# Two joins of a four-layer network in one kernel: 64-channel weights loaded early, evictions shared, transposes earlier, weight steps regrouped and wide idle products added

## The chip, the cores and the metric

The kernel runs on one core of a Trainium2 chip. The metric is the device time of one execution in microseconds (us). The core's engines are TensorE (PE in the profile; its weight loads are PEld), VectorE (DVE), ScalarE (ACT), GpSimd (POOL) and SyncE (SP); each works through its own list of instructions in order, and they wait for one another by semaphores. SP, ACT and POOL also issue DMA transfers (SPq, ACTq, POOLq).

## The reference

Everything is float32. The input x is 4 images of 256 channels, 56 x 56 pixels. Four residual layers follow one another; each normalises its input by groups (32 groups of 8 channels, per image) and adds its result to its input:

```python
x = x + involution0(groupnorm(x))   # h = reduce(x) 256 -> 64 channels; kernels = span(h), 16 groups of 7x7;
                                    # every pixel's 7x7 neighbourhood is weighted by its own kernels
x = x + conv(groupnorm(x))          # relu(n + bn2(conv3x3(relu(bn1(conv3x3(n))))))  with n = groupnorm(x)
x = x + involution2(groupnorm(x))   # as layer 0, with relu(bn(.)) on the 64 channels, relu(bn(.)) on the result
x = x + fourier_gates(groupnorm(x)) # n times a channel gate plus n times an image gate
```

## The kernel before

The program is one launch. `involution_layer(0)`, `conv_layer` and `involution_layer(2)` (which also does layer 3 image by image) are written one behind the other, each overlapping its end with the beginning of the next. Within a stage a function `in_order` fixes the order of instructions on each engine to that in which the Python code emits them, so an instruction waits behind everything emitted ahead of it on its engine. Small generators are stepped by hooks: `place(after, g, (1, 3, 5))` puts one step of `g` behind positions 1, 3 and 5 of a loop.

**An involution layer.** A 64-channel bottleneck comes first. `bottleneck(b)` (line 421) multiplies the 64-channel weights `red_sb` by the normalisation's scale (`redn`, line 430), finds a bias from them by a product with the shift (line 437) and an addition (`hb`, line 448), and then, for 7 pieces of 9 rows, makes products of 504 columns into one PSUM bank per pair of pieces (line 459): one piece of a pair lies in partitions 0 to 63, the other in 64 to 127. The evictions (line 478 in layer 2) are three ACT activations a piece, with relu, into `hp`; and as the taps need each piece in both halves of the partitions, a copy of 64 x 504 is made on DVE (line 467).

The tap stage (`tap_matrices`, line 569) makes the 7 x 7 weights: groups of 12 records (products of 133 columns, line 580) into two banks, evicted in turn by ACT (line 591, one group in three) and DVE (line 598, two in three) with a bias into `kt`. `z_sb` and `zb_sb` are tables for these products, read back from memory at the beginning of layer 2 (lines 952, 953). The windows `xw` of the image are made beside them: `next_strip` (line 362) writes a normalised strip (line 379 by ACT in layer 2, line 381 by POOL in layer 0), `begin_windows` (line 390) transposes it by 7 products with a unit matrix (line 396), and `next_windows` copies it out by ACT (line 408) and issues four DMAs by SP. Three windows are made ahead (`NXW = 3`), by hooks at groups 2, 7 and 12 of the first tap stage. `apply` (line 622) then multiplies taps and windows, and lines 635 to 647 evict that and add the residual.

**The convolution.** Both 3 x 3 convolutions are done in positions: along x a transform of the input turns 4 columns of output into 6 positions, taken in the order 1, 2, 3, 4, 0, 5. `phases` (line 1274) writes the input's normalised phases `ph` by ACT (line 1290, 8 of them), `input1` (and `input2` for the second convolution) with the transform (lines 1293 to 1320) compute `v`, one tile a position, on DVE: lines 1298 to 1302 end the first position, lines 1304 to 1320 the others; line 1318 ends the one that `conv2`'s first products wait for. `row_weights` (line 1201) makes the weights' positions on DVE, per half `ci` of the input channels: two additions (1218, 1219) and a subtraction (1220) for the first positions, three more operations (1223 to 1225) for the later ones; `u_sb` holds them. It runs as `weights1` for the first convolution (products in line 1411) and as `weights2` for the second (line 1493), the latter stepped at positions 3, 5, 7, 9 and 11 of the first chunk of `conv1`. DVE also evicts the products: lines 1432 to 1440 in `conv1`, 1503 to 1530 in `conv2`, the last piece of the convolution in lines 1524 to 1529.

**The first join.** At the end of layer 0, `begin_conv` (line 1145) issues the first rows of the convolution (`load_rows(0)`) and raw weights by SP. At the start of `conv_layer` (lines 1561 to 1580) TensorE makes 24 narrow products of 16 columns (`window_biases`, line 255), which are the biases of layer 2's taps; ACT copies them out and SP stores them (line 1570), then `load_rows(1)` issues four loads by SP (line 1137); DVE does the first `weights1` steps and the first `v`.

**The second join.** `begin_last` loads the first image of layer 2 into its blocks during the last steps of the convolution. `involution_layer(2)` issues the loads of `red_sb` by ACT (line 317) where the layer's tiles are made, `z_sb` and `zb_sb` by SP, then runs `bottleneck(0)` in one go, then the first strip and the taps.

Of the kernel before, what the change touches and what calls it, by code (L numbers as in the profile page):

```python
# [71 lines left out]
def net_kernel(  # L72
# [59 lines left out]
    for i in range(2):  # L132
        nc.scalar.dma_start(rp[i * R : (i + 1) * R, :], rpar)
    mhalf = const.tile([P, NB], F32, name="mhalf")
    nc.gpsimd.memset(mhalf, -0.5)
# [64 lines left out]
    def norm_steps(st, one_bank, layer, b, cb):  # L200
# [22 lines left out]
        yield  # L223

    def mark():
        return len(nc.cur_bb.bb.instructions)
# [22 lines left out]

    def window_biases(zb_sb, bias, ps):  # L250

        bias_f = bias[:G, KK * KK : KK * KK + ZN]
        for p in range(TP):
            z0 = ZF - p // TX * QX - p % TX
            nc.tensor.matmul(  # L255
                ps[:Q, p * G : (p + 1) * G],
                bias_f[:, z0 : z0 + Q],
                ident_sb[:G, :G],
                start=True,
                stop=True,  # L260
            )
        nc.scalar.copy(
            zb_sb.rearrange("q g p -> q p g"), ps[:Q, : TP * G].rearrange("q (p g) -> q p g", g=G)
        )
# [15 lines left out]
    def involution_layer(layer, xin, xout, red, span, sb, xs_of, ahead=None, pending=None):  # L280

        with ExitStack() as es:
# [23 lines left out]
            if layer == 0:  # L306
# [3 lines left out]
                nc.scalar.copy(norm_sb[:, 3, B - 1, 1, :], mhalf)  # L310

            red_sb = wpool.tile([P, NB, 2, R], F32, name="red_sb")

            def load_red():
                for i in range(2):
                    eng = nc.gpsimd if layer == 0 else nc.scalar
                    eng.dma_start(red_sb[:, :, i], red.rearrange("(cb p) r -> p cb r", p=P))

            if layer == 2:
                load_red()  # L320
            z_sb = wpool.tile([P, G // 2, ZN], F32, name="z_sb")
# [40 lines left out]
            def next_strip():  # L362
# [14 lines left out]
                img = xs_of[b, cb].rearrange("p (h w) -> p h w", w=W)[:, :, lo:hi]  # L377
                if layer == 2:
                    nc.scalar.activation(dst, img, AF.Identity, bias=shift, scale=rstd)
                else:  # L380
                    nc.gpsimd.tensor_scalar(dst, img, rstd, shift, ALU.mult, ALU.add)  # L381
# [39 lines left out]
            def bottleneck(b):  # L421
# [3 lines left out]

                rstd, shift = norms[layer][b]

                redn = work.tile([P, NB, 2, R], F32, name="redn", bufs=1)
                for ci in range(NB):
                    nc.vector.tensor_scalar_mul(redn[:, ci], red_sb[:, ci], rstd[:, ci : ci + 1])  # L430
                hp = new_h().rearrange("p (y x a t) -> p y x a t", y=TY, x=TX, t=NTX)
# [20 lines left out]
                for j in range(0, NH, 2):  # L452
                    halves = [slice(0, R), slice(R, P)] if j + 1 < NH else [slice(0, P)]
                    ps = one_bank()
                    for ci in range(NB):
                        for i, m in enumerate(halves):
# [8 lines left out]
                            )  # L465
                    for dst, part in copies:
                        nc.vector.tensor_copy(dst, part)
                    copies = []
                    s = ps[:, : ROWS_H * W].rearrange("p (a y t x) -> p y x a t", y=TY, t=NTX, x=TX)
                    for i, m in enumerate(halves):  # L470
                        rows = min(ROWS_H, H - (j + i) * ROWS_H)
                        a0, n = (j + i) * ROWS_H // TY, -(-rows // TY)
                        for py in range(min(rows, TY)):
                            dst = hp[m, py, :, a0 : a0 + n, :]
                            if layer == 0:
                                nc.scalar.activation(dst, s[m, py, :, :n, :], AF.Identity, bias=hb[m])
# [4 lines left out]
                        if len(halves) > 1:  # L481
                            part = hp[:, :, :, a0 : a0 + n, :].rearrange("p y x a t -> p (y x) (a t)")
                            copies.append((part[halves[1 - i]], part[m]))
                    yield

            def begin():
# [7 lines left out]
                next(tables)  # L494
                load_red()
                hp = new_h().rearrange("p (y x a t) -> p y x a t", y=TY, x=TX, t=NTX)
# [7 lines left out]
                sums0, sums1 = sums(0, 0), sums(0, 1)  # L504
                redn = work.tile([P, NB, 2, R], F32, name="redn", bufs=1)
                rstd, shift = norms[0][0]
# [443 lines left out]
            else:  # L950
                since = mark()
                nc.sync.dma_start(z_sb, z2_dram)
                nc.sync.dma_start(zb_sb, zb2_dram)
                run(bottleneck(0))
                hooks0[3] = list(pending[0])
            next_strip()
            for i in range(NXW):
                hooks0.setdefault(2 + 5 * i, []).extend((next_windows, next_strip))

# [185 lines left out]
    def begin_conv():  # L1145
        room["v2"] = new_block()
        load_rows(0, src[1])
        raw_weights(1, 0, 1, nc.sync)

    def begin_weights(part):  # L1150
# [4 lines left out]
    def conv_layer(xin, xout, st, ahead):  # L1155
        with ExitStack() as es:
# [44 lines left out]
            def row_weights(u, wc, raw=None):  # L1201
# [15 lines left out]
                for w0, w1, w2, u1, u2, u3, u4 in ws:  # L1217
                    tt(u2, w0, w2, ALU.add)
                    tt(u1, u2, w1, ALU.add)
                    tt(u2, u2, w1, ALU.subtract)  # L1220
                    yield
                for w0, w1, w2, u1, u2, u3, u4 in ws:
# [345 lines left out]
            zb2 = room["bias"][:Q, KK * KK + ZN : KK * KK + ZN + G * TP].rearrange("p (g t) -> p g t", g=G)  # L1568
            window_biases(zb2, room["bias"], one_bank())
            nc.sync.dma_start(zb2_dram, zb2)  # L1570
            load_rows(1, xin)
            g = input1(0)
            for _ in range(4):
                next(g)
            run(weights1)
            run(g)
# [73 lines left out]
    def begin_last():  # L1650
        for cb in range(NB):
            blocks[0, cb] = new_block()
            load_block(blocks[0, cb], src[2][0][cb])

    pending = conv_layer(src[1], src[2], st, begin_last)
# [66 lines left out]
```

## Time and profile before

| quantity | value |
|---|---|
| runs of the kernel before (us) | 1819.07, 1824.24, 1819.11, 1819.72; median 1819.42 |
| the profiled execution | 1819.07 us, of which 1817.3 from its first to its last instruction |
| busy share: PE, DVE, ACT, POOL | 95%, 76%, 46%, 24% |
| granted TensorE clock, mean | 0.98 of full speed |
| the first join | about 505 to 592 us |
| the second join | about 1239 to 1292 us |

The profile's times are us from the span's first instruction. Its views: the chain that ended last gives, in order of time, the start of a piece, its length and what it was (engine, tile, line, number of instructions); the timeline gives groups of instructions, with the idle time of the engine ahead of them and what ended it in square brackets; the windows give for a stretch each engine's busy time and the TensorE clock that was granted, as a share of full speed. A float32 product shows as several matmul records. Line numbers are those of the kernel before.

### The profile page before, as it was taken

What the parts mean: (1) busy time and instruction counts of PE and PEld (TensorE: products, weight loads), DVE (VectorE), ACT (ScalarE), POOL (GpSimd) and SP (SyncE); (2) the same over time, 40 slices, a digit from 0 to 9 for tenths busy, and PEclk for the clock granted to TensorE, in tenths of its full rate; (3) what the DMA queues carried; (4) which work ended last, traced back from release to release, by engine and by line L of the source; (5) the groups of instructions that cost most, each with busy time, mean ns of one, the idle gap of its engine ahead of it and who ended that gap; (6) DMA issues with size and microseconds to landing.
All of it is one profiled execution on the core that took longest, in us unless ns stands there. A gap on an engine that the chain in (4) does not pass through costs nothing.

```text
span 1817.3 us, 55835 instructions
## 1 busy us (share of the span) xinstructions
PE 1719.0 (95%) x24034; PEld 1512.1 (83%) x24034; DVE 1375.1 (76%) x2729; ACT 843.5 (46%) x1981; POOL 431.4 (24%) x626
## 2 busy tenths in 40 slices
PE   7999999999989999999999999996999899899897
PEld 6998889889878988998899889984987787787785
DVE  3787777776689988898888988874777577677675
ACT  3566556555533222322222212103767567577564
POOL 2333432245200000000000000000000465474582
PEclk9999999999989999999999999998999999999996
DMA  2545534454651101111111111131434566665653
GB/s 85 160 154 161 169 115 149 149 158 134 197 176 45 63 26 63 67 64 40 62 60 59 60 41 34 37 131 57 158 130 144 171 200 201 185 222 172 178 157 114
DMA packets 66004, 215.77 MB, mean 119 GB/s; under 512 B 13237, under 2 KB 20926, under 8 KB 62046
## 3 DMA queue, kind: packets, MB, share of 16 engines
q1 hardware_dynamic: 48718, 145.24, 25.3%
q0 software_dynamic: 14688, 64.78, 11.2%
q8 instruction: 190, 3.11, 0.7%
q10 hardware_dynamic: 2352, 2.18, 0.4%
q14 instruction: 56, 0.46, 0.1%
HBM read 76.30 MB, written 49.15 MB: 69 GB/s over the span
## 4 chain that ended last, share of the span: by engine, by line
PE 78%; DVE 8%; ACT 5%; DMA 4%; issue 2%; POOL 2%; SPq 1%; POOLq 0%; ACTq 0%; DVEq 0%
PE mm L1493 20%; PE ps L580 17%; PE ps L622 14%; PE mm L1411 10%; PE mm L1382 5%; PE ps L396 5%; DMA xw<-xw 3%; ACT kt L591 2%; PE ps L459 2%; DVE un L642 1%; DVE kt L598 1%; ACT xw L408 1%; PE ps L705 1%; PE ps L928 1%; PE ps L255 1%
## 5 line engine op out<-in xcount | busy, mean ns | idle before, releaser
L622 PE MATMUL ps<-kt,xw 126*32 126x48 f32 (+1 forms) x12544 | 378.2, 234 | 30.0 <-issue 20.7
L580 PE MATMUL ps<-hp,z_sb 64*126 64x133 f32 x6144 | 390.3, 281 | 16.1 <-ACT kt L591 8.2
L622 PEld LDWEIGHTS ps<-kt,xw 126*32 126x32 f32 (+1 forms) x12544 | 340.2, 121 | 74.8 <-issue 53.7
L580 PEld LDWEIGHTS ps<-hp,z_sb 64*126 64x126 f32 x6144 | 368.0, 187 | 33.8 <-ACT kt L591 14.4
L1493 PE MATMUL mm<-v,u_sb 128*128 128x280 f32 (+1 forms) x1728 | 385.0, 384 | 3.4 <-DVE v L1318 3.4
L598 DVE TENSOR_TENSOR kt<-ps,zb_sb 126x798 f32<-126x798 f32 x336 | 319.9, 982 | 89.9 <-PE ps L580 89.3
L1493 PEld LDWEIGHTS mm<-v,u_sb 128*128 128x128 f32 x1728 | 327.5, 190 | 57.9 <-DVE v L1318 3.8
L591 ACT ACTIVATE kt<-ps,zb_sb 126x133 f32<-126x133 f32 x1056 | 307.4, 444 | 93.7 <-PE ps L580 93.1
L1411 PE MATMUL mm<-v,u_sb 128*128 128x252 f32 (+1 forms) x936 | 212.0, 387 | 2.6 <-DVE v L1302 2.6
L1411 PEld LDWEIGHTS mm<-v,u_sb 128*128 128x128 f32 x936 | 177.8, 191 | 33.2 <-issue 2.6
L1530 POOL DMA_DIRECT2D x<-xs x24 | 13.1, 547 | 682.8 <-DVE xs L1529 427.3
L642 DVE SCALAR_TENSOR_TENSOR un<-ps,s,un 128x240 f32<-128x240 f32 x224 | 102.5, 457 | 88.2 <-ACT un L637 84.1
L642 DVE SCALAR_TENSOR_TENSOR un<-ps,par_sb,un 128x240 f32<-128x240 f32 x224 | 98.1, 457 | 87.2 <-ACT un L635 82.7
L1478 ACT ACTIVATE res<-xs,shift,norm_sb 128x1120 f32<-128x1120 f32 (+1 forms) x24 | 30.2, 1258 | 234.9 <-DVE xs L1529 107.2
L408 ACT COPY xw<-ps 126x896 f32<-126x896 f32 x112 | 101.5, 906 | 46.8 <-PE ps L396 37.5
L647 POOL TENSOR_TENSOR xs<-un,xs 128x240 f32<-128x240 f32 x112 | 72.3, 665 | 193.4 <-DVE un L642 193.4
L396 PE MATMUL ps<-ident_sb,strip_sb 128*126 128x128 f32 x784 | 110.6, 281 | 6.6 <-POOL strip_sb L381 6.1
L635 ACT ACTIVATE un<-ps,par_sb 128x240 f32<-128x240 f32 x112 | 50.2, 449 | 115.8 <-PE ps L622 113.8
L637 ACT ACTIVATE un<-ps,bn_t,s 128x240 f32<-128x240 f32 x112 | 60.2, 538 | 88.5 <-PE ps L622 79.6
L1382 PE MATMUL mm<-xs,u_sb 128*128 128x126 f32 (+1 forms) x792 | 98.5, 277 | 1.2 <-DVE xs L1345 0.9
L396 PEld LDWEIGHTS ps<-ident_sb,strip_sb 128*126 128x126 f32 x784 | 84.1, 141 | 17.5 <-POOL strip_sb L381 7.3
L139 POOL TENSOR_TENSOR norm_sb<-norm_sb,mhalf 128x1 f32<-128x1 f32 x32 | 19.8, 620 | 329.5 <-DVE norm_sb L138 329.5
(254 smaller groups left out, 2005.6 us busy)
## 6 DMA issues: line engine op xcount, KB each, us to landing
xw<-xw SPq DMA_DIRECT2D x168, 252.0 KB
xw<-xw SPq DMA_DIRECT2D x224, 126.0 KB
xw<-xw POOLq DMA_DIRECT2D x56, 252.0 KB, 4.7
xs<-x SPq DMA_DIRECT2D x24, 560.0 KB
x<-xs POOLq DMA_DIRECT2D x8, 1568.0 KB, 8.3
xs<-x SPq DMA_DIRECT2D x8, 1568.0 KB
xs<-in_x_dram SPq DMA_DIRECT2D x6, 1568.0 KB
x<-xs SPq DMA_DIRECT2D x6, 1568.0 KB
```

The costliest lines, as they stand in the source:

```text
L396: nc.tensor.transpose(ps[:Q, k * P : (k + 1) * P], flat[:, k * Q : (k + 1) * Q], ident_sb)
L408: nc.scalar.copy(xw[:, :NSB, :], ps[:Q, : NSB * P].rearrange("q (n c) -> q n c", n=NSB))
L580: nc.tensor.matmul(ps[:Q, i, k * NT : (k + 1) * NT], z_sb[i * R : (i + 1) * R, cb * GB // 2 + gp, z0 : z0 + Q], hp[i * R : (i + 1) * R, py ...
L591: nc.scalar.activation(kt[:, g0 + i, pb, :, k], ps[:Q, i, k * NT : (k + 1) * NT], AF.Identity, bias=zb_sb[:, cb * GB + g0 + i, p0 + k : p0 ...
L598: nc.vector.tensor_tensor(kt[:, g0 : g0 + 2, pb], ps[:Q, :, : PB * NT].rearrange("q i (k t) -> q i t k", k=PB), zb_sb[:, cb * GB + g0 : cb ...
L622: nc.tensor.matmul(v[m * j : m * j + m, i, :, k * TP : (k + 1) * TP], xw[:, window(ty), m * j : m * j + m], kt[:, ng * j : ng * j + ng, :, ...
L637: nc.scalar.activation(part, o[0], AF.Identity, bias=bn["t4"][:, cb : cb + 1], scale=bn["s4"][ng][:, 0, cb : cb + 1])
L642: nc.vector.scalar_tensor_tensor(part, o[e], s, part, ALU.mult, ALU.add)
L647: nc.gpsimd.tensor_tensor(dst, u, dst, ALU.add)
L1382: nc.tensor.matmul(ps[:, co * m : (co + 1) * m], u[ci][:, co * P : (co + 1) * P], v2[:, e, : n // 2, ci * WT : (ci + 1) * WT], start=(ci = ...
L1411: nc.tensor.matmul(ps, u1_sb[:, ci, dy, k, co * P : (co + 1) * P], v[:, k, dy * NB + ci : (dy + n - 1) * NB + ci + 1 : NB, :], start=(j == 0),
L1493: nc.tensor.matmul(ps, u2_sb[:, ci, dy, k, co * P : (co + 1) * P], v[:, k, dy * NB + ci : (dy + n - 1) * NB + ci + 1 : NB, :], start=(j == 0),
```

## The change

*Ahead of layer 2.* `red_sb` becomes a tile that lives for the whole program, filled for layer 2 by SP at the end of layer 0. Its scaling (`redn`) is done in `begin_last` during the convolution's last steps.

*Bottleneck of the first image of layer 2.* Of a pair of pieces, ACT evicts the first (three activations), DVE the second by three multiply-and-add operations and a maximum with zero. ACT makes one of the two copies, DVE the other.

*First windows of layer 2.* The first strip is written ahead of the bottleneck, and two of the three windows are transposed and copied between the bottleneck and the taps; the third stays at hook 7. The first two strips are made by POOL.

*Start of the convolution.* In `row_weights` both halves' first weights (additions) come first and both subtractions in a step of their own, behind the third step of the first `v`. Between the narrow bias products 12 wide ones of 448 columns are put, a unit matrix times rows of the input, into a bank that nobody reads. For `weights2` the step more means that its later operations move behind the `v` of the same position.

```diff
@@ -131,6 +131,16 @@
     rp = const.tile([P, 5], F32, name="rp")
     for i in range(2):
         nc.scalar.dma_start(rp[i * R : (i + 1) * R, :], rpar)
+
+    red_sb = const.tile([P, NB, 2, R], F32, name="red_sb")
+
+    def load_red(red, eng):
+        for i in range(2):
+            eng.dma_start(red_sb[:, :, i], red.rearrange("(cb p) r -> p cb r", p=P))
+
+    def new_redn():
+        return const.tile([P, NB, 2, R], F32, name="redn")
+
     mhalf = const.tile([P, NB], F32, name="mhalf")
     nc.gpsimd.memset(mhalf, -0.5)
 
@@ -222,6 +232,14 @@
         nc.vector.scalar_tensor_tensor(shift, gm, -1.0, rstd, ALU.mult, ALU.mult)
         yield
 
+    redn_of = {}
+
+    def norm_weights(layer, b):
+
+        redn = redn_of[layer, b] = new_redn()
+        for ci in range(NB):
+            nc.vector.tensor_scalar_mul(redn[:, ci], red_sb[:, ci], norms[layer][b][0][:, ci : ci + 1])
+
     def mark():
         return len(nc.cur_bb.bb.instructions)
 
@@ -247,7 +265,7 @@
         copy(field(bias_f), bias_g.rearrange("p (y x) -> p y x", y=KK))
         yield
 
-    def window_biases(zb_sb, bias, ps):
+    def window_biases(zb_sb, bias, ps, between=None):
 
         bias_f = bias[:G, KK * KK : KK * KK + ZN]
         for p in range(TP):
@@ -259,6 +277,8 @@
                 start=True,
                 stop=True,
             )
+            if between is not None and p % 2:
+                between()
         nc.scalar.copy(
             zb_sb.rearrange("q g p -> q p g"), ps[:Q, : TP * G].rearrange("q (p g) -> q p g", g=G)
         )
@@ -308,16 +328,6 @@
                 load(0, 1, (2, 2, 2, 1))
 
                 nc.scalar.copy(norm_sb[:, 3, B - 1, 1, :], mhalf)
-
-            red_sb = wpool.tile([P, NB, 2, R], F32, name="red_sb")
-
-            def load_red():
-                for i in range(2):
-                    eng = nc.gpsimd if layer == 0 else nc.scalar
-                    eng.dma_start(red_sb[:, :, i], red.rearrange("(cb p) r -> p cb r", p=P))
-
-            if layer == 2:
-                load_red()
@@ -375,7 +385,7 @@
                     nc.vector.memset(st[:, PAD : PAD + H, at + hi - lo : QX], 0.0)
                 dst = st[:, PAD : PAD + H, at : at + hi - lo]
                 img = xs_of[b, cb].rearrange("p (h w) -> p h w", w=W)[:, :, lo:hi]
-                if layer == 2:
+                if layer == 2 and len(strips) > 2:
                     nc.scalar.activation(dst, img, AF.Identity, bias=shift, scale=rstd)
                 else:
                     nc.gpsimd.tensor_scalar(dst, img, rstd, shift, ALU.mult, ALU.add)
@@ -423,11 +433,13 @@
 
 
 
-                rstd, shift = norms[layer][b]
-
-                redn = work.tile([P, NB, 2, R], F32, name="redn", bufs=1)
-                for ci in range(NB):
-                    nc.vector.tensor_scalar_mul(redn[:, ci], red_sb[:, ci], rstd[:, ci : ci + 1])
+                _, shift = norms[layer][b]
+
+                both = (layer, b) == (2, 0)
+
+                if (layer, b) not in redn_of:
+                    norm_weights(layer, b)
+                redn = redn_of[layer, b]
                 hp = new_h().rearrange("p (y x a t) -> p y x a t", y=TY, x=TX, t=NTX)
                 nc.gpsimd.memset(hp[:, TY - 1, :, NTY - 1, :], 0.0)
                 h_of[b] = hp
@@ -463,8 +475,11 @@
                                 start=(ci == 0),
                                 stop=(ci == NB - 1),
                             )
-                    for dst, part in copies:
-                        nc.vector.tensor_copy(dst, part)
+                    for i, (dst, part) in enumerate(copies):
+                        if both and i == 1:
+                            nc.scalar.copy(dst, part)
+                        else:
+                            nc.vector.tensor_copy(dst, part)
                     copies = []
                     s = ps[:, : ROWS_H * W].rearrange("p (a y t x) -> p y x a t", y=TY, t=NTX, x=TX)
                     for i, m in enumerate(halves):
@@ -472,7 +487,11 @@
                         a0, n = (j + i) * ROWS_H // TY, -(-rows // TY)
                         for py in range(min(rows, TY)):
                             dst = hp[m, py, :, a0 : a0 + n, :]
-                            if layer == 0:
+                            if both and i == 1:
+                                nc.vector.tensor_scalar(
+                                    dst, s[m, py, :, :n, :], bn["s3"][m], hb[m], ALU.mult, ALU.add
+                                )
+                            elif layer == 0:
                                 nc.scalar.activation(dst, s[m, py, :, :n, :], AF.Identity, bias=hb[m])
                             else:
                                 nc.scalar.activation(
@@ -481,6 +500,8 @@
                         if len(halves) > 1:
                             part = hp[:, :, :, a0 : a0 + n, :].rearrange("p y x a t -> p (y x) (a t)")
                             copies.append((part[halves[1 - i]], part[m]))
+                            if both and i == 1:
+                                nc.vector.tensor_scalar_max(part[m], part[m], 0.0)
                     yield
 
             def begin():
@@ -492,7 +513,7 @@
                 tables = span_table(z_sb, span, scratch, nc.gpsimd.dma_start, nc.scalar.copy)
                 next(biases)
                 next(tables)
-                load_red()
+                load_red(red, nc.gpsimd)
                 hp = new_h().rearrange("p (y x a t) -> p y x a t", y=TY, x=TX, t=NTX)
                 nc.gpsimd.memset(strip_sb, 0.0)
                 nc.gpsimd.memset(hp[:, TY - 1, :, NTY - 1, :], 0.0)
@@ -502,7 +523,7 @@
                 window_biases(zb_sb, scratch[:, n:], one_bank())
                 folds = batch_norms()
                 sums0, sums1 = sums(0, 0), sums(0, 1)
-                redn = work.tile([P, NB, 2, R], F32, name="redn", bufs=1)
+                redn = new_redn()
                 rstd, shift = norms[0][0]
                 steps(sums0, NCHUNK)
                 norm = norm_of(0, 0, 0, sums_of[0, 0])
@@ -951,11 +972,17 @@
                 since = mark()
                 nc.sync.dma_start(z_sb, z2_dram)
                 nc.sync.dma_start(zb_sb, zb2_dram)
+                next_strip()
                 run(bottleneck(0))
                 hooks0[3] = list(pending[0])
-            next_strip()
-            for i in range(NXW):
-                hooks0.setdefault(2 + 5 * i, []).extend((next_windows, next_strip))
+                for _ in range(NXW - 1):
+                    next_windows()
+                    next_strip()
+                hooks0[7] = [next_windows, next_strip]
+            if layer == 0:
+                next_strip()
+                for i in range(NXW):
+                    hooks0.setdefault(2 + 5 * i, []).extend((next_windows, next_strip))
 
             def last_column(sums):
                 return lambda: sums(NTX - 1)
@@ -1146,6 +1173,7 @@
         room["v2"] = new_block()
         load_rows(0, src[1])
         raw_weights(1, 0, 1, nc.sync)
+        load_red(red2, nc.sync)
 
     def begin_weights(part):
         if part == 0:
@@ -1217,8 +1245,10 @@
                 for w0, w1, w2, u1, u2, u3, u4 in ws:
                     tt(u2, w0, w2, ALU.add)
                     tt(u1, u2, w1, ALU.add)
+                    yield
+                for w0, w1, w2, u1, u2, u3, u4 in ws:
                     tt(u2, u2, w1, ALU.subtract)
-                    yield
+                yield
                 for w0, w1, w2, u1, u2, u3, u4 in ws:
                     stt(u4, w2, 4.0, w0, ALU.mult, ALU.add)
                     stt(u3, w1, 2.0, u4, ALU.mult, ALU.add)
@@ -1566,12 +1596,20 @@
             run(phases(0))
 
             zb2 = room["bias"][:Q, KK * KK + ZN : KK * KK + ZN + G * TP].rearrange("p (g t) -> p g t", g=G)
-            window_biases(zb2, room["bias"], one_bank())
+            warm_ps = one_bank()[:, : CR * W]
+
+            def warm():
+
+                nc.tensor.matmul(warm_ps, ident_sb, room["rows"][:, : CR * W], start=True, stop=True)
+
+            window_biases(zb2, room["bias"], one_bank(), warm)
             nc.sync.dma_start(zb2_dram, zb2)
             load_rows(1, xin)
             g = input1(0)
-            for _ in range(4):
+            for _ in range(3):
                 next(g)
+            next(weights1)
+            next(g)
             run(weights1)
             run(g)
             scales(0)
@@ -1651,6 +1689,7 @@
         for cb in range(NB):
             blocks[0, cb] = new_block()
             load_block(blocks[0, cb], src[2][0][cb])
+        norm_weights(2, 0)
 
     pending = conv_layer(src[1], src[2], st, begin_last)
     involution_layer(2, src[2], src[3], red2, span2, sb2, blocks, pending=pending)
```

## The prediction

> **What bounds the kernel.** I read the shares of the chain first: TensorE carries most of it, so an edit pays only where TensorE stands still, or runs slowly, and its own work comes later for that.
>
> ```profile
> PE 78%; DVE 8%; ACT 5%; DMA 4%; issue 2%; POOL 2%; SPq 1%; POOLq 0%; ACTq 0%; DVEq 0%
> ```
>
> The edits touch two joins. The chain of waits at the second (convolution to layer 2; start, us, what):
>
> ```profile
> 1240.00 0.46 DVE xs L1524
> ...
> 1242.87 0.41 ACTq L317
> 1243.32 5.92 DMA red_sb<-in_red_dram
> ...
> 1249.38 0.98 PE ps L437 x4
> 1250.36 3.58 PE ps L459 x8
> ...
> 1262.21 4.36 PE ps L580 x36
> ...
> 1277.97 13.54 PE ps L580 x228
> 1291.51 0.58 PE ps L396 x4
> ```
>
> Three things stand one behind the other: a weight load, the bottleneck product at half clock (3.58 us for 8 records), and 8 us until the taps begin at 1262.21. The timeline says what those 8 us are:
>
> ```profile
> 1254.02 8.36 ACT L478 ACTIVATE hp<-ps,hb,bn_s 64x168 f32<-64x168 f32 x20 [22.12 <-PE ps L459]
> 1255.30 0.42 DVE L467 COPY hp<-hp 64x504 f32<-64x504 f32 x1 [4.68 <-ACT hp L478]
> ```
>
> One ACT row of 20 activations, 0.42 us each, end to end, while DVE does one copy per three.
>
> The first join (layer 0 to convolution), from the timeline:
>
> ```profile
> 507.34 8.15 PE L255 MATMUL mm<-ident_sb,xs 16*126 16x16 f32 x48 [1.05 <-DVE un L642]
> 508.24 6.61 ACT L1290 ACTIVATE ph<-xs,norm_sb 128x294 f32<-128x294 f32 x8 [1.42 <-POOL xs L647]
> 515.57 0.80 DVE L1298 SCALAR_TENSOR_TENSOR v<-ph 128x616 f32<-128x616 f32 x1
> 517.11 0.80 DVE L1302 TENSOR_TENSOR v<-v 128x616 f32<-128x616 f32 x1
> 518.06 36.85 PE L1411 MATMUL mm<-v,u_sb 128*128 128x280 f32 x144 [2.57 <-DVE v L1302]
> ```
>
> TensorE does 24 narrow bias products (48 records), then waits for DVE's first position. The windows (stretch, us, PE, PEld, DVE, ACT, POOL busy, granted clock, ...) show the price: the clock is halved with the array busy throughout, and comes back only within 523–524.
>
> ```profile
> 508.00:509.00 1.00, 1.00 (x11) 1.00 (x11) 0.63 (x1) 0.76 (x1) 0.70 (x2) 1.00 0.00 0
> 510.00:511.00 1.00, 1.00 (x6) 1.00 (x7) 0.97 (x4) 1.00 (x2) 0.13 (x3) 0.50 0.68 178
> 523.00:524.00 1.00, 1.00 (x5) 0.78 (x4) 0.97 (x2) 0.19 (x1) 0.00 (x0) 0.79 0.00 0
> ```
>
> The clock's record puts the halves at 509.78–523.43. The narrow records came 0.11 us apart before, 0.21 after.
>
> **Second join, part by part.** *Weights ahead.* The two loads of `red_sb` go to SP at the end of layer 0; SP issues nothing from 463.7 to 480, two issues by SP cost about 1.3 us (L1206 and L1207: 0.64, 0.61), and nobody is queued. `redn`'s two multiplies (L430, 0.48 us together) go into the convolution's last steps, beside products of TensorE. Cover gone, they cost 0.5 us; I take nothing. TensorE's first product then waits only for the last DVE reading of the convolution's PSUM, L1524, ending 1240.45. So it starts at 1240.55 instead of 1249.38, 8.8 us sooner. The clock is still full: TensorE paused 0.6 us. The 28 records come at 0.23 us each (an L459 row further on: 8 in 1.84 us), the first 8 by 1242.7 and then at 1244.6 and 1246.4.
>
> But the evictions need `hb`, and DVE's order puts it behind work that does not move: L1525, L1486 and L1527, then L1529 until 1244.14, L222 twice, the strip's memset (L373, 0.20) and `hb` itself (L448, 0.22): about 1244.7. What is late next is therefore DVE, and 2 us of the 8.8 are lost.
>
> *Shared evictions.* Of each pair of halves ACT takes one (3 activations, 0.42 each, 1.25 us), DVE the other: three `tensor_scalar` and a `max`. No row has these. Bounds: per `tensor_scalar` 0.27 us (64x168 by L467's 0.42 us for 504 columns, with a fixed part) to 0.45 (L1524, 280 columns from PSUM); for the `max` 0.42 (L467) to 0.69 (L1233, 512 columns). In the built order DVE's first waits for ACT's third of the same bank, ACT's copy of the duplicate (0.42–0.55) waits for the `max`, and ACT's next group comes behind that copy. So the halves are serial: 1.25 + 0.82 to 1.35 + 0.42 to 0.69 + 0.42 to 0.55 = 2.9 to 3.8 us a group. Three groups and a last half of 0.84 make 9.6 to 12.3. I take 10.0, near the low end since L467 is the same shape: last write at 1244.7 + 10.0 = 1254.7, taps from there. Before, ACT alone needed 8.07 us (1254.02–1262.09), so this edit *costs* 2 us here. Together the taps start at 1254.75 instead of 1262.21, 7.5 us sooner; by the high end 1257, 5.2.
>
> *First transposes sooner.* Two of three transpose blocks (L396, 7 records, 1.41 and 0.92 us on the chain) move to TensorE's idle time before the taps; their strips go to POOL (L381, 1.01 us), idle but for an issue of 0.58. Behind them two ACT copies (L408, 0.91) and a strip (1.04) stand ahead of ACT's first tap eviction (L591, 1.65): it ends near 1259.65, and TensorE's fourth group needs it. From 1254.75 the first 36 records take 4.36 cold, so that wait is about 0.5 us. Five groups of 12 by about 1264.4 at the cold rate; the 24 left at 0.713 each (13.54 us for 19) take 17.1, with up to 0.9 of the third transpose between: the tap stage ends at 1281.5 to 1282.4 instead of 1291.51. Gain 9.1 to 10.0, I take 9.5; with the slow evictions 7, with fast ones 11.
>
> **First join, part by part.** *One position's weights first.* Moving the two subtractions (L1220, 0.96 each) behind L1302 would give 1.9 us, but DVE then reaches L1298 at 513.6 and needs ACT's eight phases, which end at 514.85 (508.24 + 6.61). L1302 ends at 517.25, 0.65 sooner; every later `v` is 1.28 later.
>
> *Wide idle products.* 12 products of 448 columns, two records each at 0.38 (L1411's 280 columns take 0.236 at full clock), go between the 24 narrow ones: 12 x (4 x 0.11 + 2 x 0.38) = 14.4 us from 507.34, so to 521.7. The convolution's first product is 3.6 us later than 518.06 but at full clock. Before, 5.37 us of it (518.06–523.43) ran at half, worth 2.7. Net +0.9. The clock should hold: taking each record's columns at full rate (448 in 0.38 us), they fill 0.45 of the stretch 506.4–509.8 after which it fell. Worked out in the same way for the stretches before each other change of the clock, 0.09 to 0.39 lost it, and 0.37 and 0.57 kept it.
>
> The Trainium skill (TensorE: Matmul & The Clock Gate, Part 1: The HAM clock gate) says that the gate watches how busy the array has been over free-running windows of about 3.4 us and throttles after an idle one. Read by it alone, the array was busy from 507.34 to 515.49, the clock should have held, and the wide products are pure delay: +3.6 us instead of +0.9. The rows differ: 0.50 at 510–511 with the array 1.00 busy, so here columns streamed count, not busy time.
>
> *Queues.* SP's `load_rows(1)` (four loads from 517.04) is now behind the bias store, which waits for the last product: issued near 522.5, landing 526.3 to 528 by its 18 us for four with the first two needed at about 529.3: hidden by 1.5 us. Cover gone, 1 to 3.
>
> *Later weights in their own step.* This stretch is DVE's: the chain from 549.28 to 590.65 has hardly anything else.
>
> ```profile
> 588.37 0.60 DVE hp L1437
> 588.99 0.68 DVE last_y L1438
> 590.00 0.60 DVE v L1318
> 590.65 24.65 PE mm L1493 x120
> ```
>
> L1318 comes three weight operations sooner (2.9 us), but the second half of that position still needs its weights at 590.6, by when half the products are fed: 1.1 us, between 0 and 2.9. First join: +0.9 - 1.1, about zero; bounds -3 to +3.
>
> **Sum.** The profiled execution's time is 1819.07 (span 1817.3 and 1.8 around it), 0.35 under the median of four. 1819.07 - 9.5 + 0.0 = 1809.6.
>
> **Rivals.** (A) *The idle products run at half clock* (slower than before). If the window to 509.8 is not full enough, ten groups of 4 x 0.21 + 2 x 0.76 = 2.36 us follow: to 533.5, and the convolution begins at half as well. Against 520.8 (518.06 + 2.7) that is +12.7, with another cold window +15.4; less 9.5: 1822 to 1825, I say 1824.6. It decides if the convolution's first product starts after 530.3. For it: stretches filled to 0.49 and 0.55 at half clock did not rise. Against it: 0.45 lies above every stretch that fell.
> (B) *Evictions side by side*: ACT and DVE overlap on the two halves, some 1.3 us a group less: 1805.5. Nothing in the order speaks for it.
> The Trainium skill (PSUM — Partial Sum Buffer, PSUM bank collisions raise a hardware error) says that two engines may access one bank at once in different 32-partition quadrants; partitions 0–63 and 64–127 are such, so by it B needs no new hardware, but no run here shows it.
> (C) *Eviction chain at its high end*, with ACT's copies ahead of taps eating more: 7 us gained, 1812.
> (D) *The first wait is only renamed*: TensorE's first product waits for a bank or for strips until about 1247, or the weights arrive no sooner: 4 to 5 us left, 1815. The order speaks against it.
>
> **Chances.** Forecast 0.60; A 0.13; B 0.10; C 0.11; D 0.06. The range 1804 to 1816 holds all but A and the tails. 0.2% (3.6 us) is about what a measurement of this kernel tells from no change: faster takes forecast, B, C and most of D, 0.82; same 0.07 (rest of D, A half realised); slower 0.11.
>
> **What would show it.** Right: no wait of L437's product for a DMA, first product at about 1240.5 on this time base; evictions of one group about 3.1 us; tap products from 1254.7; full clock from 507 to 524 and L1411 beginning near 521.7. Wrong: a clock of 0.50 anywhere within 510–520 (A); DVE's `tensor_scalar` rows inside ACT's activation rows (B); a wait of the first tap product above 10 us from `hb` (C); a gain in layer 2 given back before its end.

## The result, and the profile after

The changed kernel took 1824.84 us (median of 51 runs, 1805.67 to 1838.04), the kernel before 1818.3 (77 runs, 1806.86 to 1827.1) beside it; the ratio is 1.0018, 95% interval 1.0005 to 1.0031. So it is slower by a little, where 1809.6 was forecast. (The comparison leaves out the longest executions; the two medians by themselves give 1.0036.)

The median hides what happened. With each run goes the mean TensorE clock of that execution, and the 51 runs fall into two groups by it: 22 at a clock of 0.982 or more, median 1812.8 us, and 28 at 0.977 or less, median 1829.1; one lies between, at 0.979. The profiled execution, 1833.27 us with a span of 1831.5, is of the second group. The shares of its chain show DVE up from 8 to 10%:

```profile
PE 76%; DVE 10%; ACT 5%; DMA 4%; issue 3%; POOL 2%; SPq 1%; POOLq 0%; ACTq 0%; DVEq 0%
```

**The first join.** The timeline (start, us, engine, line, operation, tiles, shapes, count):

```profile
509.36 0.61 PE L273 MATMUL mm<-ident_sb,xs 16*126 16x16 f32 x4 [1.40 <-DVE un L663]
509.90 1.02 PE L1603 MATMUL mm<-xs,ident_sb 128*128 128x448 f32 x2
...
513.17 1.03 PE L273 MATMUL mm<-ident_sb,xs 16*126 16x16 f32 x4
514.13 1.86 PE L1603 MATMUL mm<-xs,ident_sb 128*128 128x448 f32 x2
...
518.50 0.80 DVE L1332 TENSOR_TENSOR v<-v 128x616 f32<-128x616 f32 x1
...
540.51 4.74 PE L1441 MATMUL mm<-v,u_sb 128*128 128x280 f32 x16
```

The first group of narrow and wide products takes 1.49 us (509.36 to 510.85), the later ones 2.75 (513.17 to 515.92): the clock was lost in the second. DVE has the first position of `v` at 519.3, but the convolution's first product comes at 540.51, 31.2 us after the join's start; before, 10.7. The windows (stretch, us, then PE, PEld, DVE, ACT, POOL busy, granted clock) show TensorE busy without a break at half clock, on to the end of the products:

```profile
512.00:514.00 2.00, 2.00 (x6) 0.83 (x4) 1.97 (x5) 2.00 (x4) 0.25 (x5) 0.50 0.94 320
526.00:528.00 2.00, 2.00 (x7) 1.05 (x5) 1.97 (x3) 0.00 (x0) 0.00 (x0) 0.50 0.00 0
```

**The second join.** The wait for a DMA is gone. One group of shared evictions, from the chain of waits, and the taps' start:

```profile
1258.43 0.46 DVE xs L1554
...
1263.09 1.26 ACT hp L497 x3
1264.35 0.03 issue
1264.37 1.23 DVE hp L491 x3
1265.60 0.02 issue
1265.62 0.43 DVE hp L504
1266.06 0.02 issue
1266.08 0.63 ACT hp L480
1266.71 0.01 issue
1266.72 1.26 ACT hp L497 x3
...
1274.45 8.21 PE ps L601 x96
```

ACT, DVE, DVE, ACT stand one behind the other, 3.63 us a group. Measured from the start of the convolution's last product to that of the first product of taps and windows (L622 before, L643 after), the second join takes 43.5 us (1257.99 to 1301.47); before, 52.8 (1239.56 to 1292.35). The forecast gain is there, 9.3 us, and more than that was lost ahead of it. What follows took 530.0 us in this profile and 525.0 before; in the ten other profiles it took 520.0 to 530.4, so two profiles can't show whether a few us are given back there. By its times the kernel with only the second join's edits (below) is 0.54% faster, some 9.8 us, and so loses little of the gain.

### The profile page after: what moved, and what is told of

The parts are those of the page before. It is cut to its first block, busy times and chain, and to the rows that moved or that the text cites. A ratio compares the mean times of both kernels' runs of the same rounds, so it can differ in the third digit from the quotient of the medians.

```text
span 1831.5 us, 55889 instructions
## 1 busy us (share of the span) xinstructions
PE 1744.0 (95%) x24058; PEld 1524.0 (83%) x24058; DVE 1375.3 (75%) x2738; ACT 840.1 (46%) x1973; POOL 432.3 (24%) x628
## 4 chain that ended last, share of the span: by engine, by line
PE 76%; DVE 10%; ACT 5%; DMA 4%; issue 3%; POOL 2%; SPq 1%; POOLq 0%; ACTq 0%; DVEq 0%
PE mm L1523 18%; PE ps L601 17%; PE ps L643 15%; PE mm L1441 10%; PE mm L1412 5%; PE ps L406 5%; DMA xw<-xw 3%; ACT kt L612 2%; DVE un L663 1%; PE ps L471 1%; PE mm L1603 1%; DVE kt L619 1%; DVE res L1516 1%; DVE xs L1375 1%; ACT xw L418 1%
## 5 line engine op out<-in xcount | busy, mean ns | idle before, releaser
L643 PE MATMUL ps<-kt,xw 126*32 126x48 f32 (+1 forms) x12544 | 381.2, 236 | 30.0 <-issue 17.4
L643 PEld LDWEIGHTS ps<-kt,xw 126*32 126x32 f32 (+1 forms) x12544 | 343.7, 122 | 74.5 <-issue 53.0
L601 PEld LDWEIGHTS ps<-hp,z_sb 64*126 64x126 f32 x6144 | 369.7, 187 | 33.1 <-ACT kt L612 12.7
L1412 PEld LDWEIGHTS mm<-xs,u_sb 128*128 128x128 f32 x792 | 94.4, 191 | 3.2 <-DVE xs L1428 1.6
```

What stands on the lines that cost most here:

```text
L601: nc.tensor.matmul(ps[:Q, i, k * NT : (k + 1) * NT], z_sb[i * R : (i + 1) * R, cb * GB // 2 + gp, z0 : z0 + Q], hp[i * R : (i + 1) * R, py ...
L643: nc.tensor.matmul(v[m * j : m * j + m, i, :, k * TP : (k + 1) * TP], xw[:, window(ty), m * j : m * j + m], kt[:, ng * j : ng * j + ng, :, ...
L1412: nc.tensor.matmul(ps[:, co * m : (co + 1) * m], u[ci][:, co * P : (co + 1) * P], v2[:, e, : n // 2, ci * WT : (ci + 1) * WT], start=(ci = ...
```

## The experiments

Theory 1: the wide products fill too few columns for the clock to be safe, and where its stretches of 3.41 us fall against the program decides. Theory 2: the loss lies in the moved weight steps, the early loads or the shared evictions.

**The changed kernel again** (no edit).

> The changed kernel once more, for a profile and more times. Theory 1 (the clock in the first join): the 12 wide products between narrow ones fill only about half of TensorE's columns (4 narrow records and 2 wide ones took 1.49 us at full clock, of which the wide columns are 0.75), which is too near to what the clock needs; where the stretches of 3.41 us fall against the program decides whether it holds. Then times fall into two groups, near 1812 (clock 1.00 from 509 to 525, first convolution product near 525) and near 1828 (clock 0.50 until about 540, first convolution product at 540), with little between. Theory 2 (the loss lies elsewhere, in the weight steps moved on DVE, the early loads or the shared evictions): one group, and a profile with the clock at full shows no less time than 1822.

Measured: median 1823.67 of 12 runs, ratio 1.0017 (0.9987 to 1.0047). Five runs at a clock of 0.981 or more took 1813.6 to 1821.6, four at 0.976 or less 1830.3 to 1835.1, and three at 0.977 and 0.978 took 1823.6 to 1824.0: the clock orders the times, but three runs fell into the gap between the groups, where I had expected little. The profile was one with the clock lost: groups of 2.75 us, convolution 32.1 us after the join's start. So no profile of the changed kernel itself shows a held clock; the third experiment has one.

**Without the wide products.**

```diff
...
-            window_biases(zb2, room["bias"], one_bank(), warm)
+            window_biases(zb2, room["bias"], one_bank())
```

> The changed kernel without the 12 wide products, all else kept. Theory 1: the second join's gain is left, 9.8 us measured from the last reading of the convolution's PSUM to the end of the first tap stage (51.1 to 41.3 us), and up to 1 us from the weight steps: 1818.3 - 9.8 - 0 to 1 = 1807.5 to 1808.5, in one group as wide as the kernel before's. Theory 2: no better than 1815, since the moved steps are still there.

Measured: median 1810.52 (12 runs), ratio 0.9949 (0.9925 to 0.9973), clocks 0.977 to 0.982. Taking these 12 products out of the changed kernel turns a small loss into a gain of half a per cent. It is 2 to 3 us above the number that I gave, inside a spread of 1802.7 to 1819.0. Theory 2's 1815 is not met.

**Only the wide products, in the kernel before.**

```diff
...
-            window_biases(zb2, room["bias"], one_bank())
...
+            window_biases(zb2, room["bias"], one_bank(), warm)
```

> The kernel before with nothing but the 12 wide products between its narrow ones. Theory 1: 12 groups of 1.49 us end at about 525, 4.5 us later than the half clock cost before: 1823; or the clock is lost and 12 groups of 2.75 us end near 540: 1837. Two groups, none at 1818. Theory 2: the products lie in TensorE's idle time, 1818 to 1820.

Measured: median 1827.71 (12 runs), ratio 1.006 (1.0029 to 1.009). Six runs from 1823.3 to 1826.5 at a clock of 0.980 or more, one at 1829.0, five from 1834.8 to 1843.2 at 0.975 or less: the two groups, from this edit alone. Its profile caught the clock held (the same windows as above):

```profile
512.00:514.00 2.00, 2.00 (x11) 1.24 (x10) 1.93 (x5) 2.00 (x3) 0.00 (x0) 1.00 0.94 341
526.00:528.00 2.00, 2.00 (x8) 1.42 (x8) 2.00 (x4) 1.10 (x1) 0.00 (x0) 1.00 0.02 4
```

Twelve groups of 1.49 us then end 17.7 us after the join's start. Even the lucky case loses 4 to 5 us: the second kind of convolution product (L1382 before), in its stretch behind `conv2`'s first products, starts 112.1 us after the join's start instead of 107.8.

**Only the second join's edits.** `row_weights` and the start of the convolution are as before; the 64-channel weights, evictions and transposes as in the changed kernel.

```diff
                     tt(u1, u2, w1, ALU.add)
+                    tt(u2, u2, w1, ALU.subtract)
                     yield
-                for w0, w1, w2, u1, u2, u3, u4 in ws:
-                    tt(u2, u2, w1, ALU.subtract)
-                yield
...
```

> The kernel before with only the second join's edits (weights ahead, shared evictions, first transposes sooner); the first join is as before. Theory 1: 1818.3 - 9.8 = 1808.5, and 0 to 1 us above the kernel that also regroups the weight steps. Theory 2 in its form that the weight steps cost: 1808 here and 1815 or more with them; in its form that the early loads or the shared evictions cost: 1815 or more in both.

Measured: median 1809.68 (11 runs), ratio 0.9946 (0.9923 to 0.9969), 42.8 us from the convolution's last product to the first of taps and windows. The second join's edits bring what was forecast of them. By time the regrouped weight steps can't be told from none (1810.52 against 1809.68); Theory 2 falls as an account of the loss.

**Evictions by ACT alone** (without the wide products).

```diff
-                both = (layer, b) == (2, 0)
+                both = False
...
```

> The changed kernel without the wide products, and with the evictions of layer 2's first bottleneck by ACT alone and the copies by DVE, as before. Theory 1 (the shared evictions are serial, 3.63 us a group of which ACT's own three take 1.25): ACT alone needs 2.5 a group and 8.36 in all instead of 11.6, so the taps begin 3.2 us sooner and the time is 2 to 3 us under that of the kernel that only lacks the wide products, about 1807.5. Rival: sharing takes load off ACT, whose copies and tap evictions come next, so undoing it costs 0 to 2 us.

Measured: median 1807.55 (7 runs), ratio 0.9932 (0.9902 to 0.9962). The taps start 13.3 us after the convolution's last product, and the first product of taps and windows comes at 39.5; in the kernel that only lacks the wide products, at 16.4 and 43.9. The sharing of evictions is a part of the second join that costs; the trace shows it, and the ratios point the same way (0.9932 here, 0.9949 there) with overlapping intervals.

**Evictions shared by pairs** (without the wide products): DVE takes the second pair whole, ACT the others, DVE makes all copies.

```diff
...
-                            if both and i == 1:
+                            if both and j == 2:
                                 nc.vector.tensor_scalar(
...
-                            if both and i == 1:
+                            if both and j == 2:
                                 nc.vector.tensor_scalar_max(part[m], part[m], 0.0)
...
```

> The changed kernel without the wide products, and with the evictions shared by pairs (by PSUM bank) instead of by halves: DVE does the second pair whole, ACT the first, third and last, DVE all copies. Theory 1: ACT needs 2.5 + 2.5 + 0.7, DVE 2 x (1.22 + 0.42) and six copies of 0.42, side by side: about 6 us from the bias instead of 11.6, taps 5 us sooner, the tap stage's end 4 to 5 sooner: about 1805.5, under both kernels. Rival: ACT's two window copies and strip then stand ahead of its first tap eviction and DVE's copies end late, so that no more than 2 us is left: 1808.

Measured: median 1803.66 (6 runs), ratio 0.9905 (0.9877 to 0.9933). The timeline shows what by halves was never seen: ACT and DVE evicting at the same time, each from its own PSUM bank.

```profile
1244.57 5.80 ACT L495 ACTIVATE hp<-ps,hb,bn_s 64x168 f32<-64x168 f32 x14 [12.76 <-DVE hb L460]
1244.66 1.16 DVE L489 TENSOR_SCALAR hp<-ps,bn_s,hb 64x168 f32<-64x168 f32 x3 [0.22 <-PE ps L471]
...
1246.28 1.21 DVE L489 TENSOR_SCALAR hp<-ps,bn_s,hb 64x168 f32<-64x168 f32 x3
1247.53 0.42 DVE L502 TENSOR_SCALAR hp<-hp 64x504 f32<-64x504 f32 x1
1247.98 3.20 DVE L480 COPY hp<-hp 64x504 f32<-64x504 f32 x6
1251.28 3.01 PE L599 MATMUL ps<-hp,z_sb 64*126 64x133 f32 x48 [0.68 <-ACT xw L418]
```

From the bias to the taps it takes 6.7 us (1244.57 to 1251.28) instead of 11.4 (1263.09 to 1274.45). This kernel is faster than the one before and the changed one; against sharing by halves (0.9949) and ACT alone (0.9932) its ratio is lower too, with overlapping intervals. By halves DVE's rows waited each time for ACT's third of the same bank (L491 for L497, 4.4 us in three waits), a wait that the program has; whether two engines could read the halves of one bank at once, no run here shows.

**The same wide products ahead of the narrow ones.**

```diff
-            window_biases(zb2, room["bias"], one_bank(), warm)
+            for _ in range(TP // 2):
+                warm()
+            window_biases(zb2, room["bias"], one_bank())
```

> The changed kernel with the same 12 wide products put ahead of the 24 narrow ones instead of between them. Theory 1 (columns streamed per stretch decide): while the wide ones run back to back the clock holds in every run, 24 records of 0.38 to 0.45 make 9 to 11 us, then 48 narrow records 5 to 7: the convolution begins 14.5 to 18 us after the join's start instead of 17.9 or 30, with up to one or two stretches at half clock behind it. One group of times, 1813 to 1818, none above 1824. Rival (the number of products or the work beside them decides, not their density): two groups 16 us apart as in the changed kernel.

Measured: median 1814.37 (12 runs, 1809.6 to 1821.2), ratio 0.9964 (0.9944 to 0.9984), clocks 0.979 to 0.984: one group. The timeline:

```profile
509.16 9.29 PE L1603 MATMUL mm<-xs,ident_sb 128*128 128x448 f32 x24 [1.06 <-DVE un L663]
518.38 5.46 PE L273 MATMUL mm<-ident_sb,xs 16*126 16x16 f32 x48
523.76 21.47 PE L1441 MATMUL mm<-v,u_sb 128*128 128x280 f32 x83
```

The same 72 records take 14.6 us instead of 17.9, and a wide record 0.39 and a narrow one 0.11, near the prediction's 0.38 and 0.11. Up to `conv2` the clock fell only at 523.7, for one stretch.

**Twice as many wide products between the narrow ones.**

```diff
             if between is not None and p % 2:
                 between()
+                between()
```

> The changed kernel with two wide products after each pair of narrow ones instead of one. Theory 1: a group takes about 2.3 us at full clock, of which 1.5 are wide columns (0.64 instead of 0.50), the clock holds in every run, the products end 28 us after the join's start, and the times make one group near 1825. Rival (density does not decide): two groups, near 1825 and near 1850, where groups of 4.6 us at half clock need 55 us.

Measured: median 1826.77 (12 runs, 1819.9 to 1835.9), ratio 1.0035 (1.0013 to 1.0056), clocks 0.980 to 0.985, none near 1850. The profile shows the same 2 us as above, at full clock while the products run:

```profile
526.00:528.00 2.00, 2.00 (x9) 1.01 (x8) 1.97 (x4) 0.00 (x0) 0.00 (x0) 1.00 0.04 8
```

A group takes 2.24 us, of which wide columns are 4 x 0.38 = 1.52, a share of 0.68. With more and denser idle work no run had the low mean clock of a loss that lasts. The profile alone would not tell, since a step of the clock's record fell at 508.9, 0.2 us ahead of its products, as in the profile that kept the clock with half as many. The kernel with the wide products first has the same amount of them as the changed one, and no second group either: density decides, not the amount.

**Six wide products first**, on the kernel with evictions shared by pairs, and that kernel again beside it.

```diff
+            for _ in range(TP // 4):
+                nc.tensor.matmul(warm_ps, ident_sb, room["rows"][:, : CR * W], start=True, stop=True)
             window_biases(zb2, room["bias"], one_bank())
```

> The kernel with evictions shared by pairs and no wide products between the narrow ones, with 6 wide products put ahead of the 24 narrow ones. Theory 1: 12 records of 0.38 us and 48 of 0.11 end 10.1 us after the join's start, where the first position of v is ready anyway; the clock holds through the wide ones and is lost for at most one or two stretches in the narrow ones, so the first convolution's products from their start to the next kind of product take 35 to 37 us instead of 38.2: 1 to 3 us gained, 1801 to 1803. Rival: the narrow products lose the clock as late as matters, and nothing is gained or up to 1 us lost: 1803.5 to 1805.

> The same kernel without the 6 wide products, on the same chip beside it, so that the two can be compared: 1803.7 as measured before, between 1802 and 1806.

Measured: 1805.28 with them (ratio 0.994, 0.9916 to 0.9964), 1803.64 without (0.9934, 0.9907 to 0.996). Nothing gained. In the profile with them the clock held until 518.5 and was then at half to 525.3, just when the convolution began (519.33): the narrow products lost it anyway, only later. But that is not why nothing was gained. From the convolution's first product to the next kind of product it takes 38.20 us, where 35 to 37 were expected, and 38.18 to 38.22 in all four kernels with these weight steps and no wide products, with 2.9 to 4.9 us of the convolution at half clock: DVE sets the pace there (below, the weight steps). No filling that was tried in this join was worth its place.

## Why the prediction was wrong, point by point

**The step that failed** is "the clock should hold", in the term for the wide idle products. Rival A was given 0.13; of 51 runs 28 went its way.

Two numbers in that step were off, and one assumption. The first is the group's length: 4 x 0.11 + 2 x 0.38 = 1.20 us was taken from records that run behind their like. Where narrow and wide ones alternate a group takes 1.49, so each change of kind costs about 0.13 us ((1.49 - 2 x 0.39 - 4 x 0.11) / 2, with the records' times of the kernel that has the wide ones first), and the 12 groups 17.9 us instead of 14.4. That alone makes the net of the wide products +4 to +5 instead of +0.9 with the clock held (112.1 against 107.8). The second follows from it: the share of time in which wide columns stream is 0.76 / 1.49 = 0.51, not the 0.63 that 1.20 us gives. In the very stretch of the prediction, to 509.8 from a start at 507.34, that is 0.37 instead of 0.45, and no longer above the 0.39 that had lost the clock.

The assumption was where a stretch begins, and it is behind the two groups: the clock's record changes at steps of 3.41 us whose position is not tied to the program. In the profile with the clock held a step falls at 508.9 (a change at 502.1 and 2 x 3.41 more), 0.2 us before the join's start at 509.1, so the first stretch was full of products. In the two with the clock lost a step came 2.0 us (511.4) and 0.9 us (506.6) after the join's start; the stretch that ended there held TensorE's wait ahead of the join too. Once lost, the clock did not come back in some 30 us of products (at half clock the wide columns, taken at full rate, are 0.76 / 2.75 = 0.28); it came back at the end of a stretch that held convolution products, which are wide without exception. I had taken the position of the steps in the one profile that I had as given. It was a draw, and my range should have reached to rival A on that ground.

The profiles say what the draw is about. I worked out the share of every whole stretch in all twelve of them as the prediction did (each record's columns at 0.38 us for 448, overlaps counted once). At full clock it fell after 108 stretches, none of them filled to more than 0.41; it stayed after all that were filled to more, and after 19 between 0.35 and 0.41. The two stretches that lost it in the changed kernel were filled to 0.26 (508.0 to 511.4) and 0.40 (503.2 to 506.6). The five that began in the wide and narrow products at a held clock (508.9 to 526.0) were filled to 0.49 to 0.58. With the wide products first, a step fell 0.9 us after the join's start as well; that stretch was filled to 0.50 and kept the clock. So the pattern held the clock in each stretch that it filled; it was lost in the stretch in which TensorE's wait and the first groups stand together. At half clock the pattern fills a stretch to 0.24 to 0.36, and in no profile did the clock come back after less than 0.42.

That the array was busy 2.00 of 2.00 us at half clock speaks against reading "busy" as the rule. The Trainium skill (TensorE: Matmul & The Clock Gate, Part 1: The HAM clock gate) also says that the window is free-running and the effect therefore varies from run to run; that part the runs here bear out. The share does not settle every case: between 0.35 and 0.41 the clock went either way, and at half clock it sometimes stayed low up to 0.56.

**Rival A's price.** The products were to end 26.2 us after the join's start (26.0 by its own terms) and the convolution to be 12.7 to 15.4 late. With groups of 2.75 they ended after 31 us. The later kind of convolution product comes 123.3 and 126.6 us after the join's start in the two profiles, against 104.5 to 106.2 in the kernels that only lack the wide products or have other evictions besides: 17 to 22 late.

**The second join held in its sum**, with two misses that cancel. First bottleneck product 0.1 us behind the last reading of PSUM: 0.14 (1258.88 to 1259.02). Bias 4.15 us after that product: the first activation came 4.07 after. Shared evictions serial and a loss: yes, but 3.63 us a group where I took 3.05, inside the bounds of 2.9 to 3.8; the taps start 15.4 us after the first product instead of 14.2. The mis-sized pieces are the three `tensor_scalar` (1.23, near the high end of 1.35) and ACT's copy (0.63, above the 0.55 that I gave as the most). So from the convolution's last product the taps start 6.2 us sooner (16.5 instead of 22.7), not 7.5. With the transposes in TensorE's idle time, the stage from the first tap to the first product of taps and windows takes 27.0 us instead of 30.1: 3.1 gained where 2.0 were counted. Together 9.3 us by the two profiles, 10.0 with only these edits, against 9.5; that the sum fits so closely is in this part luck. Rivals B and D did not come about. Rival C half did: its sign, more than 10 us from `hb` to the first tap, showed (11.4 us even from the first activation), and its loss was made up behind it.

**The weight steps.** In the kernels that regroup them and have no wide products the convolution begins 10.1 us after the join's start instead of 10.7 (0.65 forecast), and the products from `conv2`'s first to the next kind take 31.3 to 31.4 us instead of 32.7 (1.1 forecast), or 29.7 where the clock does not dip there. Between the kernel before and the one shared by pairs, whose clocks were at half for equally long (509.8 to 523.4 and 591.7 to 595.1), the first join ends 1.65 us sooner (106.15 against 107.80). Forecast were 1.1 from the later weights; the sooner start had no term of its own in the sum.

Nor had its price, "every later `v` is 1.28 later". From the convolution's first product to `conv2`'s first it takes 64.7 us in all five kernels with the regrouped steps and no wide products between the narrow ones, with 2.9 to 6.0 us of it at half clock. With only the second join's edits it takes 63.2, with 2.9 at half. So `conv2` begins only 0.3 us sooner than before (74.8 against 75.1 after the join's start), and 0.9 later than with the old steps in that profile (73.9). The chain of waits shows the change. With the old steps (only the second join's edits) TensorE carries it:

```profile
518.68 30.00 PE mm L1439 x120
```

With the new ones (shared by pairs, the second profile) it runs over DVE, with ACT's phases between:

```profile
517.02 1.74 DVE u_sb L1248 x2
518.76 0.71 DVE v L1332
...
549.87 0.74 DVE v L1348
...
554.91 1.32 DVE xs L1373 x4
```

Where DVE carries the stretch, a faster clock in it gains nothing.

**The queue of `load_rows`.** ACT waited 0.3 us for those rows in the profile of the changed kernel and 1.6 with twice the wide products; in the others it did not wait for them. As forecast, it stayed hidden or nearly so.

## What to carry to other kernels

Idle products that are to hold the clock must be dense from the first stretch on, the one that TensorE's wait has a part in: put them back to back, or leave them out. Ask first whether TensorE carries the work behind them; here it did not, once the weight steps had moved. Count the time of a pattern from a row of that pattern, not from its parts. Where a clock's steps run free of the program, one profile shows one draw: price the loss with its own chance, and look at the times of many runs by their mean clock before trusting a median. Two engines that share a step gain nothing if the program's order makes one wait for the other; here they ran side by side when each had a bank of its own.

## What the runs showed of the hardware that had not been expected

TensorE ran for 30 us at half clock without a pause, with its array reported busy throughout; at full clock, no stretch of 3.41 us that was filled with streaming columns to more than 0.41 was followed by half clock in twelve profiles. Narrow products (16 rows, 16 columns) and wide ones (128 rows, 448 columns) cost 0.11 and 0.39 us among their like, and a change from one to the other about 0.13 us more at full clock.
